# Writing out the order of TensorE and ScalarE ahead of the first pass of a two-layer graph kernel

## The chip, the core and the metric

The kernel runs on one core of one Trainium2 chip. A core has five engines with an instruction queue each: TensorE (PE: matmuls, with weight loads shown apart as PEld), VectorE (DVE), ScalarE (ACT), GpSimd (POOL) and SyncE (SP, which here only issues DMA transfers). Each engine takes its instructions strictly in the order in which they stand in its queue, and waits on semaphores for the others. The metric is the device time of one execution in microseconds (us). The kernel before takes 966.26 us, the median of three runs (964.35 to 967.14).

## The reference

Nodes carry 128 features, there are 6250 of them and 206,250 edges, sorted by destination. Each edge also has a type from 0 to 8. Two layers are computed:

```python
deg  = segment_sum(ones, src);  norm = clip(deg, 1)**-0.5
h    = relu(layernorm(x))
x    = x + relu(segment_sum((h*norm)[src], dst)) @ W0.T + b0          # layer 0
h    = relu(layernorm(x))
msg  = h[src] @ Wmsg.T + bmsg + edge_embed[type]
x    = x + gru(segment_sum(msg, dst), h)                              # layer 1
```

## The kernel before, in words

The edges become a dense matrix of small whole numbers, 6272 by 6272 in blocks of 128 (49 blocks, `NB`). A neighbour sum is then a plain matrix product. Windows of two destination nodes each are handled side by side: an edge list is turned into two one-hot matrices (low seven bits of the source, block number of the source), and TensorE multiplies these to make columns of the dense matrix.

The program has three parts.

**The preparation** (lines 365 to 755) is what the change edits. It goes in stages.

- *Turning the edge lists.* `dst`, `src` and `etype` arrive as 128 x 1616 words (lines 374 to 377). They are cast (`dst_f`, `low_b`, `code_b`, `typ_b`, lines 425 to 435), transposed by matmuls with an identity (line 496) into six PSUM buffers, written to `turned` by ScalarE and VectorE (lines 506, 508), and stored to the DRAM table `flat` (lines 516, 521).
- *Finding the rows.* For each node pair, the place in the edge list where its edges begin is found in two steps: `less` (line 399) and the matmuls into `base_ps` (line 407) find a coarse place by counting the heads of the list, two indirect transfers fetch a `span` of 32 values around it (line 416), and `search`, `search_sums`, `last_of_search` compare and count these (lines 445 to 484). The answer is `row_i`. Between these, `stats(n)` takes the layernorm statistics of n blocks of `x` on VectorE (line 464).
- *The group loop* (lines 734 to 753). There are 25 windows, in groups of `GB` = 4. `fetch` (line 608) lets GpSimd gather the rows of a group (`got`, two buffers, line 612), VectorE compares them with the node numbers (`inside`, line 626) and masks three fields (`fields`, line 633), TensorE transposes these (line 642: 36 matmuls for a group of four windows), ScalarE writes `typ`, `code_t` and `lo_t` (lines 652, 655). `count` (line 659) then counts edge types: nine masks from `typ` (five by VectorE, line 667, four by ScalarE, line 670), ten matmuls into `sums` (lines 671, 672), two copies to `counts` by ScalarE (line 674). A *chunk* is seven blocks of nodes, which are 448 node pairs. `degrees(c)` (line 676) sums the counts of chunk c by seven matmuls (line 681), VectorE reads them (`scale`, `reach`, lines 689, 692) and ScalarE takes a root (line 693). `rows_of(c)` (line 700) makes seven normalised rows, `terms_of(c)` (line 722) rounds them into `tab1[c]`, the table of layer 0.
- *The tail.* `early_hots` (lines 747, 750) makes the first two pairs of one-hot matrices, among the last rows and terms.

**The first pass** (lines 782 to 909) goes over columns of the matrix, 128 in the first step (c = 0) and 256 in each later one. In each round `build` (line 790) makes matrix columns by 32 matmuls (line 801, into three PSUM buffers `ev`), ScalarE copies them to `adj` (line 810), and TensorE multiplies the *previous* step's columns with `tab1` (line 769, 105 matmuls a step, spread evenly over eight rounds of one step).

**The second pass** (lines 915 to 1063) reads the stored matrix again and makes layer 1.

Two things set the order of instructions. A program text in which an engine is named in `tc.manual_schedule` runs on that engine in the order in which it is written. For engines that are not named, a planner chooses the order by its own estimates. In the preparation, only VectorE is named:

```python
with tc.tile_pool(name="pro", bufs=1) as pro, tc.manual_schedule(engines={mybir.EngineType.DVE}):
...
        for i in range(NCH):
            if i >= 3:
                degrees(i - 3)
            fetch(*groups[i])
            if i >= 1:
                count(*groups[i - 1])
            if i >= 3:
                rows_of(i - 3)
                terms_of(i - 3)
```

So VectorE's share of `degrees(c)`, the instructions `scale` and `reach`, stands ahead of `inside` and `fields` of group i = c + 3, while TensorE's and ScalarE's shares stand where the planner puts them. The first pass names TensorE, ScalarE and VectorE all three. GpSimd and SyncE are planned everywhere, before and after.

Of the kernel before, what the change touches and what calls it, by code (L numbers as in the profile page):

```python
# [10 lines left out]
F32 = mybir.dt.float32  # L11
# [247 lines left out]
def by_matrix(  # L259
# [105 lines left out]
    with tc.tile_pool(name="pro", bufs=1) as pro, tc.manual_schedule(engines={mybir.EngineType.DVE}):  # L365
# [40 lines left out]
        for j in range(GT):  # L406
            nc.tensor.matmul(base_ps, less[:, j, :], one_b[:NG, :], start=(j == 0), stop=(j == GT - 1))
        base = pro.tile([P, 1], F32, name="base")
# [14 lines left out]


        dst_f = raw.tile([P, NT], F32, name="dst_f")
        nc.scalar.copy(dst_f, dst_i)
        low_i = raw.tile([P, NT], I32, name="low_i")
        nc.vector.tensor_scalar(low_i, src_i, P - 1, None, op0=ALU.bitwise_and)
# [4 lines left out]
        nc.vector.tensor_copy(code_b, src_i)  # L433
        typ_b = raw.tile([P, NT], BF16, name="typ_b")
        nc.vector.tensor_scalar(typ_b, typ_i, 0.0, float(TYPES - 1), op0=ALU.max, op1=ALU.min)
        row_i = pro.tile([P, WB], I32, name="row_i")
# [51 lines left out]
        for k0 in range(0, NT // P + 1, 4):  # L488
            k1 = min(k0 + 4, NT // P + 1)
            n = min(P, NT - k0 * P)  # L490
            for i, given in enumerate((dst_f, code_b, typ_b, low_b)):
# [17 lines left out]
            if k0 == 0:  # L509
                stats(8)  # L510
            if k0 == 4:
                search()
            if k0 == 8:
                search_sums()
# [90 lines left out]
        groups = [(b, min(GB, WB - b)) for b in range(0, WB, GB)]  # L605
        typ_of = {}

        def fetch(b0_, nb):

            got = wnd.tile([P, GB, ROWS, 4, HALF], I16, name="got")  # L610
            for b in range(nb):
                nc.gpsimd.indirect_dma_start(  # L612
                    out=got[:, b].rearrange("p r f j -> p (r f j)"),
                    out_offset=None,
                    in_=edges_flat,
                    in_offset=bass.IndirectOffsetOnAxis(ap=row_i[:, b0_ + b : b0_ + b + 1], axis=0),
                )
            typ_of[b0_] = wnd.tile([P, GB * WP], BF16, name="typ")
            w0_ = b0_ * WP
            turns_ = {i: pps.tile([P, 4, P], F32, name="turn") for i in (1, 0, 2)}  # L620
            n = nb * ROWS
            g = got[:, :nb].rearrange("p b r f j -> p (b r) f j")
            inside = wnd.tile([P, 2, GB * ROWS, HALF], BF16, name="inside", bufs=1)
            fields = wnd.tile([P, GB * ROWS, 3, 2, HALF], BF16, name="fields")
            for d in range(2):
# [5 lines left out]
                )  # L631
            for d in range(2):
# [5 lines left out]
                )  # L638
            for i in (1, 0, 2):
                for b in range(nb):  # L640
                    for r in range(ROWS):
# [6 lines left out]
                        )  # L648
            for i in (1, 0, 2):
                ws = turns_[i][:, :nb, :WP]  # L650
# [8 lines left out]
        def count(b0_, nb):  # L659
# [4 lines left out]
            for k in range(TYPES):  # L664
                if k < first_level:
                    m = wnd.tile([P, GB * WP], BF16, name="m_dve", bufs=6)
                    nc.vector.tensor_scalar(m[:, :n], typ, float(1 + k), None, op0=ALU.is_equal)  # L667
                else:
                    m = wnd.tile([P, GB * WP], BF16, name="m_act", bufs=4)
                    nc.scalar.activation(m[:, :n], typ, AF.Sign, bias=levels[:, k - first_level : k - first_level + 1])  # L670
                nc.tensor.matmul(sums_t[:both, :n], sel[:, k, :], m[:, :n], start=(k == 0), stop=False)  # L671
            nc.tensor.matmul(sums_t[:both, :n], top, ones_b[:1, :n], start=False, stop=True)
            for d in (0, 1):
                nc.scalar.copy(counts[:, b0_ * WP : b0_ * WP + n, d], sums_t[32 * d : 32 * d + rows3, :n])

        def degrees(c):
            blocks = slice(c * CB, (c + 1) * CB)
            deg = dps.tile([P, CB], F32, name="deg")
            for k in range(CB):
                w = (c * CB + k) * P // 2  # L680
                nc.tensor.matmul(
                    deg[:, k : k + 1],
# [5 lines left out]

            nc.vector.scalar_tensor_tensor(
                scale[:, blocks], deg, 1.0, dev[:, blocks], op0=ALU.max, op1=ALU.mult  # L690
            )
            nc.vector.tensor_copy(reach[:, blocks], deg)
            nc.scalar.activation(scale[:, blocks], scale[:, blocks], AF.Sqrt)

# [5 lines left out]
        def rows_of(c):  # L700

            blocks = slice(c * CB, (c + 1) * CB)
            nc.vector.reciprocal(scale[:, blocks], scale[:, blocks])
            nc.vector.scalar_tensor_tensor(
                shift_[:, blocks], mean[:, blocks], -0.5, scale[:, blocks], op0=ALU.mult, op1=ALU.mult
            )
# [7 lines left out]
            for k in range(CB):  # L714
                b = c * CB + k
                to, of, by, add = f_of[c][:, k, :], xs[:, b, :], scale[:, b : b + 1], shift_[:, b : b + 1]
                if c >= NCH - 3:
                    nc.scalar.activation(to, of, AF.Identity, bias=add, scale=by)
                else:
# [14 lines left out]
        for i in range(NCH):  # L734
            if i >= 3:
                degrees(i - 3)
            fetch(*groups[i])
            if i >= 1:
                count(*groups[i - 1])
            if i >= 3:  # L740
                rows_of(i - 3)
                terms_of(i - 3)
        degrees(NCH - 3)
        count(*groups[NCH - 1])
        rows_of(NCH - 3)
        degrees(NCH - 2)
        early_hots = [hots(0)]
        rows_of(NCH - 2)
        degrees(NCH - 1)
        early_hots.append(hots(TW, first_place[:, NB * P :]))  # L750
        rows_of(NCH - 1)
# [30 lines left out]
    with tc.tile_pool(name="adj_even", bufs=1, reuse_waits="tile") as adj_even, tc.tile_pool(  # L782
# [73 lines left out]
        for c in range(NC + 1):  # L856
# [12 lines left out]
            ends = spread(TOTAL, rounds)  # L869
# [6 lines left out]
            for r in range(rounds):  # L876
                casts = cast_at.get(r, ()) if c > 0 else ()
                for q in casts:
                    if r == 0:
                        cast(q)  # L880
                if c < NC:
# [234 lines left out]
```

## Time and profile before

| what | value |
|---|---|
| median of three runs | 966.26 us |
| the profiled execution, its own time | 970.11 us |
| the profiled execution, span from the first to the last instruction | 968.3 us |
| TensorE, ScalarE, VectorE busy in the span | 886.2, 739.8, 807.8 us |
| mean granted TensorE clock | 0.964 |
| `row_i` written (line 484) | 29.2 us after the start |
| first `inside` (line 626) | 38.2 us |
| first matmul of the first pass' sums (line 769) | 117.08 us |

The page gives busy time by engine, then the span in 40 slices of 24.2 us. In the first five slices TensorE's digits are 4, 3, 5, 6 and 4, and the granted clock's are 9, 6, 7, 7 and 5; from the sixth slice on both are 9 in nearly all slices. The preparation is thus the stretch in which no engine is full all the time. Idle time of an engine that nobody waits for costs nothing, so the busy shares are not enough; the waits and the order of the instructions in time have to be read.

### The profile page before, as it was taken

The page shows a single profiled execution, that of the slowest core. Times are in us where ns is not written, and L with a number is a line of the kernel's source. Part 1 is how long each engine was busy: PE and PEld are TensorE (multiplying, and loading weights), DVE is VectorE, ACT ScalarE, POOL GpSimd, SP SyncE. Part 2 cuts the span into 40 slices and gives each one's busy share as a digit, 9 for nine tenths or more (in the row PEclk, how much of TensorE's full clock was granted, in tenths as well). Part 3 has the DMA queues.
Part 4 walks back from the last instruction along what each step waited for, and adds up shares of the span by engine and source line. Part 5 has one row for each costly group of instructions (what it writes and reads, how often), then busy time and mean ns, then how long its engine had stood idle before and what let it go on. Part 6 is the DMA issues. An engine that isn't in the chain of part 4 may idle for free.

```text
span 968.3 us, 25145 instructions
## 1 busy us (share of the span) xinstructions
PE 886.2 (92%) x11049; PEld 735.5 (76%) x11049; DVE 807.8 (83%) x898; ACT 739.8 (76%) x1407; POOL 35.9 (4%) x73
## 2 busy tenths in 40 slices
PE   4356499999999999999999989999999999999995
PEld 3334399899899999999999878777777777777774
DVE  6969988999999999999999788987887778766753
ACT  3167889999999999999999995767577666667552
POOL 3540000000000000000000000000000000000000
PEclk9677599999999999999999999999999999999998
DMA  9430245575576576576476679877676677565530
GB/s 267 137 96 18 53 130 168 163 207 170 157 206 175 152 206 180 148 206 186 142 206 191 178 260 315 267 250 250 229 256 230 231 260 245 200 227 209 183 88 20
DMA packets 200296, 180.65 MB, mean 187 GB/s; under 512 B 10353, under 2 KB 188583, under 8 KB 200023
## 3 DMA queue, kind: packets, MB, share of 16 engines
q1 hardware_dynamic: 197938, 172.72, 57.5%
q0 software_dynamic: 1664, 4.95, 1.7%
q8 instruction: 88, 1.44, 0.6%
q10 hardware_dynamic: 576, 1.29, 0.4%
q14 instruction: 30, 0.25, 0.1%
HBM read 95.07 MB, written 83.87 MB: 185 GB/s over the span
## 4 chain that ended last, share of the span: by engine, by line
PE 74%; DVE 11%; ACT 7%; DMA 5%; issue 2%; POOL 1%; another core or an unknown queue 0%; SPq 0%; DVEq 0%; ACTq 0%
PE acc L769 52%; PE ev L801 10%; DMA piece<-adj_d 4%; DVE leave L1011 3%; PE turn L642 2%; PE gate L972 2%; PE acc L825 2%; PE gate L973 2%; DVE wide L1038 2%; ACT wide L1031 1%; ACT adj L810 1%; PE sums L671 1%; ACT f L935 1%; PE msg_ps L964 1%; PE tr L953 1%
## 5 line engine op out<-in xcount | busy, mean ns | idle before, releaser
L769 PE MATMUL acc<-wide,tab 128*128 128x256 f32 (+2 forms) x3374 | 600.1, 329 | 3.5 <-DVE wide L1038 3.4
L769 PEld LDWEIGHTS acc<-wide,tab 128*128 128x128 f32 x3374 | 492.0, 189 | 68.2 <-issue 17.7
L810 ACT CAST adj<-ev 128x784 bf16<-128x784 f32 x392 | 298.9, 820 | 30.6 <-PE ev L801 27.6
L1031 ACT ACTIVATE wide<-piece 128x512 fp32r<-128x512 bf16 (+1 forms) x336 | 201.0, 601 | 70.0 <-PE acc L769 64.0
L334 DVE TENSOR_TENSOR hot_l<-lo_t,iota 128x4096 bf16<-128x4096 bf16 x97 | 221.6, 2285 | 0.6 <-PE ev L801 0.5
L1011 DVE TENSOR_REDUCE leave<-piece 128x7 f32<-128x3584 bf16 (+2 forms) x43 | 154.9, 3602 | 47.2 <-DMA piece<-adj_d 47.2
L874 ACT CAST wide<-adj 128x1792 fp32r<-128x1792 bf16 (+1 forms) x75 | 125.2, 1669 | 0.8
L801 PE MATMUL ev<-hot_c,hot_l 64*128 64x49 bf16 x6208 | 114.2, 182 | 7.4 <-DVE hot_c L334 4.2
L801 PEld LDWEIGHTS <-hot_l 64*128 64x128 bf16 x6208 | 93.0, 93 | 36.0 <-issue 8.9
L334 DVE TENSOR_TENSOR hot_c<-code_t,iota 128x1600 bf16<-128x1600 bf16 x97 | 95.5, 985 | 0.0
L1038 DVE CAST wide<-piece 128x3584 fp32r<-128x3584 bf16 (+2 forms) x43 | 82.3, 1921 | 10.4 <-PE acc L769 10.4
L874 DVE CAST wide<-adj 128x1792 fp32r<-128x1792 bf16 (+1 forms) x75 | 81.0, 1079 | 8.7 <-ACT adj L810 7.9
L769 PE MATMUL acc<-adj,tab 128*128 128x256 bf16 x525 | 67.2, 277 | 0.5 <-ACT adj L810 0.5
L1031 ACT ACTIVATION_READ_ACCUMULATOR wide<-piece 128x1 f32 x336 | 63.2, 188 | 0.0
L769 PEld LDWEIGHTS <-tab 128*128 128x128 bf16 x525 | 48.1, 99 | 8.1 <-issue 0.6
L949 ACT COPY sum_sb<-acc 128x512 f32<-128x512 f32 (+2 forms) x13 | 7.3, 562 | 37.4 <-PE acc L769 37.4
L642 PE MATMUL turn<-ident_b,fields 128*128 128x128 bf16 x225 | 20.9, 280 | 15.4 <-DVE fields L633 15.4
L642 PEld LDWEIGHTS <-fields 128*128 128x128 bf16 x225 | 19.9, 131 | 16.1 <-issue 14.0
L612 POOL DMA_INDIRECT got<-flat,row_i x25 | 26.4, 1058 | 23.5 <-DVE m_dve L667 13.6
L972 PE MATMUL gate<-hT,whh_sb 128*128 128x512 f32 (+2 forms) x52 | 25.4, 570 | 1.2 <-DVE hT L961 1.2
L973 PE MATMUL gate<-msg,wih_sb 128*128 128x512 f32 (+2 forms) x52 | 25.3, 567 | 0.0
L980 ACT ACTIVATE rg<-gate,brz 128x512 f32<-128x512 f32 (+2 forms) x13 | 8.6, 664 | 20.0 <-PE gate L973 20.0
(160 smaller groups left out, 558.2 us busy)
## 6 DMA issues: line engine op xcount, KB each, us to landing
adj_d<-adj SPq DMA_DIRECT2D x24, 3136.0 KB
piece<-adj_d SPq DMA_DIRECT2D x77, 896.0 KB
piece<-adj_d SPq DMA_DIRECT2D x14, 672.0 KB
piece<-adj_d SPq DMA_DIRECT2D x7, 448.0 KB
out_dram<-res SPq DMA_DIRECT2D x11, 256.0 KB
xs<-in_x_dram SPq DMA_DIRECT2D x6, 448.0 KB
adj_d<-adj SPq DMA_DIRECT2D x1, 1568.0 KB
flat<-turned SPq DMA_DIRECT2D x3, 512.0 KB
```

The costliest lines, as they stand in the source:

```text
L334: nc.vector.tensor_tensor(to.rearrange("p j (k t) -> p j k t", t=2), twice.unsqueeze(2).to_broadcast([P, n, m // 2, 2]), of[:, :m].rearran ...
L612: nc.gpsimd.indirect_dma_start(out=got[:, b].rearrange("p r f j -> p (r f j)"), out_offset=None, in_=edges_flat, in_offset=bass.IndirectOf ...
L642: nc.tensor.matmul(turns_[i][:, b, :], fields[:, b * ROWS + r, i].rearrange("p d j -> p (d j)"), ident_b, start=(r == 0), stop=(r == ROWS ...
L769: nc.tensor.matmul(acc[:, : 2 * P].rearrange("f (t n) -> f t n", t=2) if twice else acc[:, :nd], tab[:, s, i, :], a[:, i, :P].unsqueeze(1) ...
L801: nc.tensor.matmul(ps[:, d, j * NB : (j + 1) * NB], hot_l[half, t, :], hot_c[half, t, :NB], start=True, stop=True,)
L810: nc.scalar.copy(adj[:, :, part * 16 : (part + 1) * 16].rearrange("p n (j d) -> p n j d", d=2), ps[:, :, : 8 * NB].rearrange("p d (j n) -> ...
L874: make(wide[q][:, :, :n], done[:, q * HP : (q + 1) * HP, :n])
L972: nc.tensor.matmul(ps[:, :nd], whh_sb[:, cols], hT[:, :nd], start=True, stop=False)
L973: nc.tensor.matmul(ps[:, :nd], wih_sb[:, cols], msg[:, :nd], start=False, stop=True)
L1011: nc.vector.tensor_reduce(leave[:, q * HP : (q + 1) * HP, c], piece, AX.X, ALU.add)
L1031: nc.scalar.activation(pieces[q][:, i, :nd], piece[:, i, :nd], AF.Copy, accum_out=leave[:, q * HP + i, c : c + 1],)
L1038: nc.vector.tensor_copy(pieces[q][:, :, :nd], piece[:, :, :nd])
```

## The change

Four edits, all ahead of the first pass but the last.

1. `tc.manual_schedule` of the preparation names TensorE and ScalarE too, so the text has to give them a good order. For this, `fetch` is split into `fetch` (GpSimd alone) and a generator `inside_of`; `count` becomes a generator; `degrees` is split into `degrees`, `scales` and `root`, and `rows_of` loses its first two instructions to `shifts`. A loop calls the pieces in turn.
2. The matmuls that count the heads (`base_ps`, line 407) stand ahead of all transposes. The casts of `dst` and the masking of `low_i` move ahead of `base`, `code_b` is cast by ScalarE in place of VectorE, the four fields are turned in the order `dst_f`, `low_b`, `typ_b`, `code_b`. `search` and `search_sums` come one quarter of the list earlier, with 4 rows of statistics in place of 8.
3. The groups have 2, 4, 4, 4, 4, 4 and 3 windows; they had 4, 4, 4, 4, 4, 4 and 1. In chunks 0 to 3 ScalarE makes 3 of the 7 rows, which VectorE made alone; in chunks 4 to 6 ScalarE makes all seven, as before.
4. In step c = 1 of the first pass, the first 35 of the 105 matmuls (line 769) stand ahead of the first `build`, and none in round 0 after it; the other 70 are spread over the seven rounds left.

```diff
-    with tc.tile_pool(name="pro", bufs=1) as pro, tc.manual_schedule(engines={mybir.EngineType.DVE}):
+    with tc.tile_pool(name="pro", bufs=1) as pro, tc.manual_schedule(
+        engines={mybir.EngineType.PE, mybir.EngineType.Activation, mybir.EngineType.DVE}
+    ):
...
         for j in range(GT):
             nc.tensor.matmul(base_ps, less[:, j, :], one_b[:NG, :], start=(j == 0), stop=(j == GT - 1))
+
+        dst_f = raw.tile([P, NT], F32, name="dst_f")
+        nc.scalar.copy(dst_f, dst_i)
+        low_i = raw.tile([P, NT], I32, name="low_i")
+        nc.vector.tensor_scalar(low_i, src_i, P - 1, None, op0=ALU.bitwise_and)
         base = pro.tile([P, 1], F32, name="base")
...
-        nc.vector.tensor_copy(code_b, src_i)
+        nc.scalar.copy(code_b, src_i)
...
-            for i, given in enumerate((dst_f, code_b, typ_b, low_b)):
+            for i, given in ((0, dst_f), (3, low_b), (2, typ_b), (1, code_b)):
...
             if k0 == 0:
-                stats(8)
+                search()
+                stats(4)
             if k0 == 4:
-                search()
-            if k0 == 8:
                 search_sums()
...
-        groups = [(b, min(GB, WB - b)) for b in range(0, WB, GB)]
+        at = [0, *range(2, WB, GB), WB]
+        groups = [(b, to - b) for b, to in zip(at, at[1:])]
...
-                if c >= NCH - 3:
+                if k in others:
                     nc.scalar.activation(to, of, AF.Identity, bias=add, scale=by)
-                else:
+                elif k in mine_:
                     nc.vector.tensor_scalar(to, of, by, add, op0=ALU.mult, op1=ALU.add)
...
+        ACT_ROWS = 3
+        fetch(*groups[0])
+        for i in range(len(groups)):
+            if i + 1 < len(groups):
+                fetch(*groups[i + 1])
+            new = inside_of(*groups[i])
+            old = count(*groups[i - 1]) if i >= 1 else iter(())
+            c = i - 3
+            run(old, 1)
+            run(new, 1)
+            if c >= 0:
+                degrees(c)
+                scales(c)
+                root(c)
+            run(new, 1)
+            run(old, 1)
+            run(new, 1)
+            if c >= 0:
+                shifts(c)
+                rows_of(c, range(ACT_ROWS, CB), range(ACT_ROWS))
+            run(new, 1)
+            run(old, 2)
+            if c >= 0:
+                terms_of(c)
...
+        old = count(*groups[NCH - 1])
+        run(old, 1)
         degrees(NCH - 3)
-        count(*groups[NCH - 1])
-        rows_of(NCH - 3)
+        scales(NCH - 3)
+        root(NCH - 3)
         degrees(NCH - 2)
+        run(old, 1)
+        shifts(NCH - 3)
+        scales(NCH - 2)
+        root(NCH - 2)
+        rows_of(NCH - 3, (), range(CB))
+        run(old, 2)
         early_hots = [hots(0)]
-        rows_of(NCH - 2)
+        shifts(NCH - 2)
+        rows_of(NCH - 2, (), range(CB))
         degrees(NCH - 1)
+        scales(NCH - 1)
+        root(NCH - 1)
         early_hots.append(hots(TW, first_place[:, NB * P :]))
-        rows_of(NCH - 1)
+        shifts(NCH - 1)
+        rows_of(NCH - 1, (), range(CB))
...
+            lead = (NARROW * SPL + 2) * HP if c == 1 else 0
+            ends = spread(TOTAL - lead, rounds) if c != 1 else [0, *spread(TOTAL - lead, rounds - 1)]
...
+                if r == 0:
+                    run(steps, lead)
                 if c < NC:
```

In the new loop the pieces of `new` (group i) are, in turn: VectorE's `inside`; then VectorE's `fields` and TensorE's transposes; then ScalarE's `typ`; then ScalarE's `code_t` and `lo_t`. The pieces of `old` (counting group i - 1) are ScalarE's four masks; VectorE's five masks; TensorE's ten matmuls; ScalarE's two copies to `counts`. Read engine by engine, an iteration with a chunk is therefore this: VectorE has `inside`, `scale`, `reach`, `fields`, five masks, the two of `shifts`, four rows, the terms. TensorE has the seven matmuls of `degrees`, the transposes, the ten matmuls of `sums`. ScalarE has four masks, the root, `typ`, three rows, `code_t`, `lo_t`, the two copies to `counts`.

## The prediction, made before the result was known

> **What bounds the kernel now.** I read the slices first, then the stage's waits, then the instructions of one iteration in time. Slices (TensorE, ScalarE, granted clock; 24.2 us each):
>
> ```profile
> PE   4356499999999999999999989999999999999995
> ...
> ACT  3167889999999999999999995767577666667552
> ...
> PEclk9677599999999999999999999999999999999998
> ```
>
> From the sixth slice on TensorE is full at the full clock, so the rest of the kernel starts when the preparation lets it and moves with it one to one. Everything below asks when TensorE's unbroken run begins (now 116.31 us, the first `ev` of c = 1). Who waits between 30 and 120 us (total, times, longest):
>
> ```profile
> PE turn L642 <- DVE fields L633: 15.4, 3, 13.5
> ...
> PE deg L681 <- ACT counts L674: 7.1, 5, 2.8
> DVE scale L689 <- PE deg L681: 7.0, 1, 7.0
> ...
> ACT lo_t L655 <- remote: 3.3, 1, 3.3
> ```
>
> VectorE loses 7.0 us once, up to 62.97, waiting for the first degrees. After that it hardly waits: the timeline has `inside` of three groups starting at 73.61, 82.24 and 90.88, that is every 8.6 us, with VectorE busy without a gap. One such iteration, in order of time (start, length):
>
> ```profile
> 82.10 0.16 DVE L689 SCALAR_TENSOR_TENSOR scale<-deg,dev 128x7 f32<-128x7 f32 x1
> ...
> 83.18 2.62 DVE L633 TENSOR_TENSOR fields<-got,inside 128x2304 bf16<-128x2304 int16 x2
> ...
> 84.89 1.42 ACT L674 CAST counts<-sums 27x500 bf16<-27x500 f32 x2
> ...
> 86.36 0.27 PE L681 MATMUL deg<-ones_b,counts 9*128 9x1 bf16 x5 [1.70 <-ACT scale L693]
> ...
> 86.57 3.78 PE L642 MATMUL turn<-ident_b,fields 128*128 128x128 bf16 x36
> ...
> 90.28 1.24 PE L671 MATMUL sums<-m_dve,sel 128*59 128x500 bf16 x5
> ...
> 90.73 0.16 DVE L689 SCALAR_TENSOR_TENSOR scale<-deg,dev 128x7 f32<-128x7 f32 x1
> ```
>
> The point to see: the degrees that VectorE reads at 90.73 were ready at 86.6, some 4 us early. The planner had let TensorE run `degrees` ahead.
>
> **Part by part: the lookup (to 29 us).** `less` ends at 8.26. `base_ps` (0.61) then follows at once and not at 11.34 behind the transposes; `base` and the two places take 0.8, so the two span transfers are issued at 10.2 and 12.5 instead of these:
>
> ```profile
> 12.82 2.03 POOL L416 DMA_INDIRECT span<-in_dst_dram,base_i  x1 [6.42 <-DVE base L422]
> ...
> 15.15 1.64 POOL L416 DMA_INDIRECT span<-in_dst_dram,base_i  x1 [0.30 <-issue]
> ...
> 21.24 1.82 DVE L446 TENSOR_TENSOR is_less<-span,nodes 128x1600 bf16<-128x1600 int32 x1
> ```
>
> By the trace's landing records they completed at 19.58 and 20.98, 6.8 and 5.8 us after issue, while the loads of `x` keep the DMA engines full; with the same delay the second lands at 18.3. `low_i` ahead of `base` costs nothing: `src_i` landed at 5.47, and its 1.0 us hides the matmuls. VectorE gives up `code_b` (1.0) to ScalarE and is through the first quarter at 14.2, so it now waits 4.1 us in `search` for the span. Behind that stand what used to be done meanwhile: 1.8 `is_less`, 0.8 for four rows of statistics, 1.3 second quarter, 2.3 `search_sums`, 1.3 and 0.5 last quarters, 0.3 `row_t`, 2.2 eleven rows, 0.15. `row_i` comes at 18.3 + 10.65 = 28.95, against 29.34: a gain of 0.4. Were the span to land with the `got` delay of 3.3 us (the chain of waits, 38.39), it would be 2.5 more; as late as now, a loss of 2.3. I keep the row of the span itself. The stores of `flat` are not ahead of their old times: SP is issuing loads of `x` up to 16.9. 34 rows of statistics instead of 30 follow (34 x 0.196 = 6.7), then eleven small instructions (2.95): `inside` of group 0 starts at 38.6, was 38.20. The small first group, landed by about 34, is not waited for at all.
>
> **The first groups.** Two windows cost about 0.62 + 1.42 on VectorE (between the rows of one window, 0.42 + 0.82, and of four, 1.03 + 2.62). `fields` of group 0 ends at 40.6 (was 41.76), and frees the buffer for group 2, which takes 7.6 us from there (now 42.03 to the `inside` at 49.68): 48.4. `inside` and `fields` of group 2 end at 52.1. TensorE's stretch on a full group, 36 transposes and ten `sums` matmuls, is the deciding size; I call it x. Four are on the timeline: 57.20 to 62.67, 66.80 to 72.58, 77.22 to 84.53, 86.57 to 92.69, so 5.5, 5.8, 7.3 and 6.1, mean 6.2. It ends at 58.3; two copies to `counts` (1.4), the last `deg` (0.3) and `scale` with `reach` (0.25) bring `fields` of group 3 to 60.2. It is 64.12 now: a gain of 3.9, from the 7.0 us wait.
>
> **The loop.** Here the gain goes. With a first group of two, groups end at 250, 750, 1250, 1750 pairs; chunks end at 448, 896, 1344, 1792. Each of chunks 0 to 3 now reaches into group c + 1 (before, group c sufficed), which is counted at the very end of the previous iteration. And VectorE meets `scale` ahead of `fields`. So the order closes a ring: `fields` 2.6, x 6.2, `counts` 1.4, `deg` 0.3, `scale` 0.25, next `fields`: 10.75 us, with TensorE idle for 4.5 of it. VectorE alone would need 7.8 (8.6 less 3 x 0.27 for the rows given away), ScalarE 8.0 (6.8 + 3 x 0.4): the rows moved to ScalarE lie in waits and are worth nothing. Three turns: `fields` of group 6 starts at 60.2 + 32.2 = 92.4, now 91.21.
>
> [...] The row: transposes follow each other every 0.107 us up to 69.5 and every 0.056 after it, as the granted clock goes from 0.5 to 1.0. [...]
>
> **The tail.** Group 6 has three windows instead of one: `fields` 2.0 and 27 transposes with `sums` of group 5 5.3 (99.7), `counts` 1.4 (101.1). ScalarE then stands with the four masks of group 6 ahead of the root of chunk 4: about 2.15 (between 1.27 for one window and 2.6 for four), 103.3. Root, shifts, `scale`, root: 1.0 (104.3). Seven rows 2.8, `counts` of three windows 1.1, seven rows 2.8, root 0.2: 111.2. VectorE is in the second pair of one-hots until 112.0 and `shifts` until 112.4; the last rows end at 115.2, and only then come all eight `adj` copies (8 x 0.725 = 5.8, from 4.35 for six): 121.0. Now:
>
> ```profile
> 111.08 4.35 ACT L810 CAST adj<-ev 128x784 bf16<-128x784 f32 x6
> ...
> 116.31 0.84 PE L801 MATMUL ev<-hot_c,hot_l 64*128 64x49 bf16 x32 [2.45 <-DVE hot_c L334]
> ```
>
> The copies end at 115.43, two of eight having been done earlier, between rows.
>
> **The 35 matmuls ahead.** They need the copies, not the one-hots, so TensorE starts at 121.05 and not 2.45 us of `hot_c` later: the run begins 4.75 us later than now, this gain counted. In the rounds left TensorE needs 0.58 + 10 x 0.13 = 1.9, ScalarE 1.53 and a cast in some: about 0.4 lost at the end. If one-hots bound, it would be up to 2.
>
> **Sum.** -0.4 (lookup) is inside the chain above, which ends 4.75 + 0.4 = 5.1 later. The profiled span of 968.3 becomes 973.4 (its own time 970.11 becomes 975.2). That execution lies 3.9 above the median 966.26, so the median becomes 971.4.
>
> **Rivals.** *Late completions too.* ScalarE's `lo_t` waited until 53.90 for transposes that by the records ended at 47.86, and once more at 72.11 for some ended at 70.2. I can't say why. Off the ring this cost little; on it, 3.3 and 1.9 us come on top: 976.6. For it: both are in the trace. Against: the two iterations after show none.
> [...]
> [...]
> The edits not being what they say is not a rival I can price: where GpSimd's planned order differs, the lookup's ends above hold it.
>
> **Numbers.** What this kernel's measurement tells from no change is about 0.3%, 2.9 us. The ring as worked out: 0.50, with its own range 968.5 to 975; late completions or the rule's 7.0: 0.18; cancelled 0.15; clock holds 0.17. A little of the first falls within 0.3%: slower 0.64, same 0.19, faster 0.17. Range 962 to 979: it holds the cancelled case, most of the slow ones, and the edge of the fast one.
>
> **What would show it.** Right: between 60 and 95 us VectorE waits on `deg` in `scale` some 2 us in every iteration, `inside` starts 10 to 11 us apart, the `deg` matmuls wait for `counts`, `search` waits 4 us for its transfer, the eight `adj` copies stand in one row. Wrong: `inside` 8.6 us apart or less, or a clock of 1.0 from 45 to 95 us.

## The result, and the profile after

The changed kernel takes 976.43 us (median of four runs, 974.70 to 979.16); the kernel before took 966.21 us in the same series (964.35 to 967.14). The ratio is 1.0111, with a 95% interval of 1.0083 to 1.0139: 10.2 us slower. The prediction was 971.4 us with a range of 962 to 979. The direction was right and the time lies in the range, but only half of the loss was foreseen (5.1 us).

The profiled execution of the changed kernel took 976.74 us by its own time, with a span of 974.7 us. Its page, in slices of 24.4 us (TensorE, ScalarE and the granted clock):

```profile
PE   3356599999999999999999979999999999999995
...
ACT  3277879999999999999999994866667657667562
...
PEclk9587699999999999999999999999999999999998
```

TensorE's fifth digit is a 5 where it was a 4, and from the sixth slice on it is full, as before; slices of 24 us are too coarse to show when the unbroken run begins. The timeline has it: it begins at 119.11 us, with the first of the 35 matmuls, and began at 116.31 before. By the stages below, all but 0.6 us of the difference lies ahead of some 142 us. The waits between 30 and 120 us (total, times, longest):

```profile
PE turn L649 <- DVE fields L639: 25.8, 7, 12.1
...
DVE scale L712 <- PE deg L700: 11.9, 5, 3.7
...
PE deg L700 <- ACT counts L692: 9.0, 6, 2.5
ACT counts L692 <- PE sums L689: 8.0, 6, 2.3
```

VectorE had waited once for degrees, for 7.0 us. Now it waits five times, 11.9 us in all, and the three other rows are the rest of the same circle: `turn` waits for `fields` (12.1 of the 25.8 us are the wait for the very first `fields`), `counts` for `sums`, `deg` for `counts`, and `scale` for `deg`. One turn of it, in order of time (start, length, in brackets the wait just before):

```profile
79.03 1.42 ACT L692 CAST counts<-sums 27x500 bf16<-27x500 f32 x2 [2.34 <-PE sums L689]
80.50 0.20 PE L700 MATMUL deg<-ones_b,counts 9*128 9x1 bf16 x2 [1.31 <-ACT counts L692]
80.74 0.17 DVE L712 SCALAR_TENSOR_TENSOR scale<-deg,dev 128x7 f32<-128x7 f32 x1 [3.15 <-PE deg L700]
80.89 2.62 DVE L639 TENSOR_TENSOR fields<-got,inside 128x2304 bf16<-128x2304 int16 x2
...
83.57 4.02 PE L649 MATMUL turn<-ident_b,fields 128*128 128x128 bf16 x36 [2.87 <-DVE fields L639]
...
88.55 1.22 PE L688 MATMUL sums<-m_dve,sel 128*59 128x500 bf16 x5
...
90.12 1.42 ACT L692 CAST counts<-sums 27x500 bf16<-27x500 f32 x2 [1.51 <-PE sums L689]
91.60 0.17 PE L700 MATMUL deg<-ones_b,counts 9*128 9x1 bf16 x1 [1.29 <-ACT counts L692]
91.81 0.17 DVE L712 SCALAR_TENSOR_TENSOR scale<-deg,dev 128x7 f32<-128x7 f32 x1 [2.49 <-PE deg L700]
```

From `scale` to `scale` it is 11.07 us (91.81 - 80.74). In the kernel before the degrees had been ready 4 us ahead; here each link waits for the one before it.

For the comparison by stage I use a second profiled execution of the kernel before, which the first experiment brought; why, it will show. The predicted column is put together from the prediction's own times.

| stage, us | before, profile shown | before, taken again | predicted | after |
|---|---|---|---|---|
| start to `fields` of group 3 | 64.1 | 61.2 | 60.2 | 58.5 |
| `fields` of group 3 to that of group 6 | 27.1 | 27.1 | 32.2 | 33.5 |
| from there to the end of the eighth `adj` copy | 24.2 | 22.5 | 28.6 | 27.1 |
| from there to the end of the last (105th) matmul of c = 1 | 20.7 | 20.3 | 20.2 | 23.2 |
| the rest of the span | 832.2 | 831.8 | 832.2 | 832.4 |
| span | 968.3 | 962.9 | 973.4 | 974.7 |

Against the undisturbed execution the change gains 2.7 us ahead of the loop, then loses 6.4 in the loop, 4.6 in the tail and 2.9 in c = 1; with 0.6 in the rest this is 11.8 us of span, near the 10.2 us by which the medians differ.

### The profile page after: what moved, and what is told of

It is laid out like the page before. It is cut to its first block, busy times and chain, and to the rows that moved or that the text cites. A ratio compares the mean times of both kernels' runs of the same rounds, so it can differ in the third digit from the quotient of the medians.

```text
span 974.7 us, 25146 instructions
## 1 busy us (share of the span) xinstructions
PE 892.2 (92%) x11049; PEld 738.9 (76%) x11049; DVE 803.3 (82%) x885; ACT 745.4 (76%) x1420; POOL 35.2 (4%) x73
## 4 chain that ended last, share of the span: by engine, by line
PE 73%; DVE 12%; ACT 7%; DMA 4%; issue 2%; POOL 1%; SPq 0%; DVEq 0%; POOLq 0%; ACTq 0%
PE acc L826 51%; PE ev L858 10%; DMA piece<-adj_d 4%; DVE leave L1072 3%; PE turn L649 2%; ACT adj L867 2%; PE gate L1033 2%; PE gate L1034 2%; DVE fields L639 2%; PE acc L882 2%; DVE wide L1099 2%; PE sums L688 1%; ACT f L996 1%; ACT wide L1092 1%; PE msg_ps L1025 1%
## 5 line engine op out<-in xcount | busy, mean ns | idle before, releaser
L858 PEld LDWEIGHTS <-hot_l 64*128 64x128 bf16 x6208 | 92.6, 93 | 31.1 <-issue 8.0
L649 PE MATMUL turn<-ident_b,fields 128*128 128x128 bf16 x225 | 22.3, 289 | 25.8 <-DVE fields L639 25.8
L649 PEld LDWEIGHTS <-fields 128*128 128x128 bf16 x225 | 20.7, 135 | 26.7 <-DVE fields L639 14.5
L664 ACT CAST typ<-turn 128x500 bf16<-128x500 f32 (+2 forms) x7 | 3.7, 532 | 31.0 <-DVE inside L630 24.5
L617 POOL DMA_INDIRECT got<-flat,row_i x25 | 26.5, 1060 | 20.2 <-DVE m_dve L684 10.0
```

Of the source, the lines that this page charges most:

```text
L617: nc.gpsimd.indirect_dma_start(out=got_of[b0_][:, b].rearrange("p r f j -> p (r f j)"), out_offset=None, in_=edges_flat, in_offset=bass.In ...
L649: nc.tensor.matmul(turns_[i][:, b, :], fields[:, b * ROWS + r, i].rearrange("p d j -> p (d j)"), ident_b, start=(r == 0), stop=(r == ROWS ...
L858: nc.tensor.matmul(ps[:, d, j * NB : (j + 1) * NB], hot_l[half, t, :], hot_c[half, t, :NB], start=True, stop=True,)
```

## The experiments

The theory to test (A in the expectations): a ring of dependences, closed by the first group of two, costs the loop and the tail their time; the 35 matmuls ahead of c = 1 cost some 3 us more; and the profile shown of before contained a stall of some 5 us that ordinary executions do not have. They ran in three series, each on a chip of its own and with its own runs of the kernel before; a ratio is always to those. The first has the second profile of before, "without the lead", "groups of four" and "degrees behind"; the second has "only VectorE's part", "the lead alone", "equal groups, no lead" and the first try with added matmuls; the third has the other four. The changed kernel itself was timed only in the measurement above, so every distance to it in time goes across series. Every profile of the second and third series holds such a stall too, so there the stages say more than the times.

**The kernel before, profiled again.** No edit.

> The kernel before, unchanged, for a second profile. The medians differ by 10.2 us (976.4 against 966.2) but the two profiled spans by only 6.4 (974.7 against 968.3). Theory A: the first profiled execution of the kernel before carried a stall of its own (ScalarE's lo_t released at 53.9 us, 6 us after its transposes), which ordinary executions lack. Then in this profile the wait of VectorE for the first degrees is 2 to 4 us instead of 7.0, fields of group 3 starts near 60 instead of 64.1, and the span is near 965. Theory B: the stall belongs to the kernel; it is there again, fields of group 3 starts near 64 and the span is near 968.

It took 964.72 us with a span of 962.9. ScalarE in the timeline of the profile shown of before ("remote" is a release that the trace puts down to no engine of this core):

```profile
53.90 0.99 ACT L655 CAST lo_t<-turn 128x1000 bf16<-128x1000 f32 x1 [3.32 <-remote]
...
60.24 0.58 ACT L652 CAST typ<-turn 128x500 bf16<-128x500 f32 x1
```

The same `typ` of group 2 in the new execution, and then VectorE's `scale` and `fields`:

```profile
55.08 0.57 ACT L652 CAST typ<-turn 128x500 bf16<-128x500 f32 x1 [0.90 <-ACT m_act L670]
...
60.04 0.17 DVE L689 SCALAR_TENSOR_TENSOR scale<-deg,dev 128x7 f32<-128x7 f32 x1 [5.50 <-PE deg L681]
...
61.19 2.62 DVE L633 TENSOR_TENSOR fields<-got,inside 128x2304 bf16<-128x2304 int16 x2
```

The wait put down to "remote" is gone, `typ` of group 2 starts 5.2 us earlier, `fields` of group 3 2.9 and the eighth `adj` copy ends 4.7 us earlier. So one program has executions with and without a stall around 50 to 60 us. The profile shown of before had it; the profile of after has no such wait. Which of the two is the ordinary execution, two profiles can't prove: the 23 runs of before in this series lie between 963.10 and 970.39 us, with the median at 966.95, and this execution lies 2.2 us below that.

**Without the lead.** The 35 matmuls ahead of c = 1 are not set in front; all else is the change.

```diff
-lead = (NARROW * SPL + 2) * HP if c == 1 else 0
-ends = spread(TOTAL - lead, rounds) if c != 1 else [0, *spread(TOTAL - lead, rounds - 1)]
+lead = 0
+ends = spread(TOTAL, rounds)
```

> The changed kernel without its fourth part: in step c = 1 the 105 matmuls are spread over the eight rounds again. Theory A (the 35 matmuls ahead cost time: ScalarE and VectorE stand idle while they run, later the matmuls run into casts that are placed for the old spread, and the clock falls): step c = 1, 23.1 us long in the changed kernel, takes 19.7 as in the kernel before, the run begins 1 us later, so 2 to 2.5 us less than the changed kernel, about 974. Theory B, the prediction's step (they fill the wait for the one-hots and cost 0.4): 0.6 to 1 us more than the changed kernel, about 977.

975.10 us, ratio 1.0079 (1.0052 to 1.0106): 2 to 3 us less than the change (8.2 us above its own median of before, not 10.2; by the ratios 3.1 us), though the intervals overlap. The stage says it better: c = 1 took 21.1 us from the last copy instead of 23.2. The lead costs time and gains none.

**Groups of four from the start.**

```diff
-at = [0, *range(2, WB, GB), WB]
+at = [*range(0, WB, GB), WB]
```

> The changed kernel with the old groups of 4, 4, 4, 4, 4, 4 and 1 windows and nothing else different. Theory A (the first group of two makes each chunk reach into the group counted last, which closes a ring of fields, transposes, sums, counts, degrees and scale): without it VectorE does not wait for degrees, inside starts about 8.3 us apart in place of 10.5 to 11.9, and the time is 6 to 9 us below the changed kernel, 967 to 970. Theory B (the written order itself is slow, ScalarE's queue being the longest): inside stays 10 us apart or more, and the time is within 2 us of the changed kernel.

970.72 us, ratio 1.0042 (1.0031 to 1.0053), which is 6.7 us better than the change. The last three turns of the loop, VectorE's timeline:

```profile
71.05 0.15 DVE L712 SCALAR_TENSOR_TENSOR scale<-deg,dev 128x7 f32<-128x7 f32 x1
71.20 2.61 DVE L639 TENSOR_TENSOR fields<-got,inside 128x2304 bf16<-128x2304 int16 x2
...
80.73 0.17 DVE L712 SCALAR_TENSOR_TENSOR scale<-deg,dev 128x7 f32<-128x7 f32 x1 [0.92 <-PE deg L700]
80.89 2.62 DVE L639 TENSOR_TENSOR fields<-got,inside 128x2304 bf16<-128x2304 int16 x2
...
88.37 0.17 DVE L712 SCALAR_TENSOR_TENSOR scale<-deg,dev 128x7 f32<-128x7 f32 x1
```

The waits of `scale` are 0, 0.92 and 0 where the change has 0, 3.15 and 2.49, and `fields` of group 3 to that of group 6 takes 28.6 us, not 33.5. With equal groups a chunk never reaches into the group that is counted last, and the ring is open. This edit alone brings back 4.9 of the 6.4 us lost in the loop. It brings back part of the tail too, 24.8 us where the change has 27.1 and the undisturbed kernel before 22.5: the last group has one window again and not three. The lead is still in this kernel: c = 1 took 24.8 us.

**Degrees behind the transposes.** In each iteration `degrees`, `scales` and `root` stand behind `fields` and its transposes, not ahead of them.

```diff
+run(new, 1)
 if c >= 0:
     degrees(c)
     scales(c)
     root(c)
-run(new, 1)
 run(old, 1)
```

> The changed kernel, but the degrees, scale and root of a chunk stand behind fields and the transposes of the iteration, not ahead of them; groups of 2, 4, ..., 3 kept. Theory A (the ring through scale sets the iteration): VectorE no longer waits 2.5 to 3.7 us in scale ahead of fields; the iteration is then set by ScalarE's own 8.0 us, so inside starts 8 to 8.5 us apart, and the end comes 8 to 10 us earlier, 966 to 968. Theory B (ScalarE's or TensorE's queue sets it whatever stands where): the wait only moves to another instruction, and the time is within 2 us of the changed kernel.

979.36 us, ratio 1.0120 (1.0095 to 1.0145). The expectation of a gain was missed. The edit made another ring: VectorE's `scale` now waits for `deg` matmuls that stand behind TensorE's 36 transposes, 15.4 us in all, and `inside` starts at 66.90, 79.06 and 91.60, some 12.3 us apart. It was a badly made test, and says only what it cost here that VectorE waits for TensorE directly after giving it 36 transposes.

**Only VectorE's part behind.** `degrees` stays ahead of the transposes, `scales` and `root` go behind `fields`.

```diff
 if c >= 0:
     degrees(c)
-    scales(c)
-    root(c)
 run(new, 1)
+if c >= 0:
+    scales(c)
+    root(c)
```

> The changed kernel, but VectorE's scale and reach, and the root, stand behind fields, while TensorE's degrees stay ahead of the transposes. The run with everything behind the transposes only made another ring: VectorE waited in scale for transposes of its own fields, inside 12.2 us apart. Here neither holds. Theory A (the ring through scale and fields sets the iteration): what is left of it on TensorE and ScalarE is counts 1.4, deg 0.3, transposes and sums 6 to 6.6, so inside starts 8 to 8.6 us apart, fields of group 6 starts 5 to 7 us earlier than 91.97, time 969 to 971. Theory B (in a written order each engine waits for another somewhere, whatever is moved): inside 10 us or more apart, time 975 to 979.

977.58 us, ratio 1.0096 (1.0072 to 1.0121), 1.4 us better than the change's ratio, within the intervals, and not the 969 to 971 expected. The ring is open all the same: the later `inside` are 8.55 and 9.31 us apart, and from `fields` of group 4 to that of group 6 it takes 17.65 us, where the change takes 23.01. But this profile has the stall again (TensorE and ScalarE, in order of time):

```profile
54.99 0.27 PE L649 MATMUL turn<-ident_b,fields 128*128 128x128 bf16 x2 [1.08 <-issue]
56.41 0.37 PE L649 MATMUL turn<-ident_b,fields 128*128 128x128 bf16 x2 [1.15 <-issue]
...
58.57 0.58 ACT L664 CAST typ<-turn 128x500 bf16<-128x500 f32 x1 [1.72 <-remote]
...
63.68 0.99 ACT L667 CAST lo_t<-turn 128x1000 bf16<-128x1000 f32 x1 [1.90 <-remote]
```

`typ` of group 2 comes at 58.57 and not at 53.88, and `fields` of group 4 at 76.07 and not at 68.96. The 5.4 us won in two turns, and more, are lost ahead of them. A kernel further below that has the stall and still the ring ("the lead with the casts moved too") takes 21.6 us for these two turns, so the stall is not what shortened them. Two edits at different links of the ring, this and the equal groups, each shorten the loop: on the path the ring is thus the cause. In the total its price can't be read from this run.

**The lead alone.** The kernel before, with the 35 matmuls put ahead of c = 1 as the change does.

```diff
-ends = spread(TOTAL, rounds)
+lead = (NARROW * SPL + 2) * HP if c == 1 else 0
+ends = spread(TOTAL - lead, rounds) if c != 1 else [0, *spread(TOTAL - lead, rounds - 1)]
...
+if r == 0:
+    run(steps, lead)
```

> The kernel before with the fourth part of the change alone: 35 of the 105 matmuls of step c = 1 ahead of the first build. Theory A (they cost): step c = 1, 20.3 us from the last adj copy to its 105th matmul in the second profile of the kernel before, takes 23 to 25; TensorE waits for a cast in the third round and the clock falls once; 969.5 to 971. Theory B, the prediction's (they fill the 2.45 us wait for the one-hots): 964 to 966.

972.33 us, ratio 1.0030 (1.0015 to 1.0045), that is about 3 us slower; c = 1 took 23.1 us. Its timeline (TensorE, then the three engines behind it):

```profile
114.81 4.64 PE L769 MATMUL acc<-adj,tab 128*128 128x256 bf16 x21 [1.62 <-ACT adj L810]
...
121.78 4.50 ACT L810 CAST adj<-ev 128x784 bf16<-128x784 f32 x6 [6.05 <-PE ev L801]
...
123.06 2.29 DVE L334 TENSOR_TENSOR hot_l<-lo_t,iota 128x4096 bf16<-128x4096 bf16 x1 [3.38 <-PE ev L801]
...
127.17 0.97 PE L769 MATMUL acc<-wide,tab 128*128 128x256 f32 x6 [1.58 <-ACT wide L875]
```

While TensorE works off the lead it makes no `ev`, so ScalarE stands 6.05 us and VectorE 3.38; what they would have done is missing later, and at 127.17 TensorE waits for a cast. The stretch starts earlier and ends later. The fall of the clock that was expected did not come: from 122.95 us on ten `acc<-wide` matmuls take 1.45 to 1.64 us each time, where ten of the changed kernel take 2.14 as its clock falls to 0.50. The lead moves TensorE's matmuls ahead and leaves the casts that feed the others in their old rounds.

**The lead with the casts moved too.** The change, with c = 1's casts one round earlier.

```diff
 cast_at = {0: (1, 2), 2: (3,), 3: (4,), 4: (5,), 5: (6,)}
+CAST_1 = {0: (1, 2, 3), 2: (4,), 3: (5,), 5: (6,)}
...
-casts = cast_at.get(r, ()) if c > 0 else ()
+casts = (CAST_1 if c == 1 else cast_at).get(r, ()) if c > 0 else ()
```

> The changed kernel with the 35 matmuls ahead kept, but the casts of step c = 1 issued sooner: blocks 1, 2 and 3 ahead of the first round, 4 and 5 in the third and fourth. Theory A (the loss of the lead is the wait for casts placed for the old spread, and the clock falling behind it): no wait for a cast in step c = 1, no fall of the clock at 132, the step 23.2 us long becomes 20.5 to 21.5, 974 to 975. Theory B (the loss is that ScalarE and VectorE idle for the 5 us of the lead and have to make it up): the step stays at 22.5 to 23.5 and the time at 976.

979.52 us, ratio 1.0096 (1.0075 to 1.0117), not the 974 to 975 expected. c = 1 took 21.3 us and no longer 23.2; TensorE no longer waits for `wide` in it. The granted clock, which in the change fell to 0.50 from 132.3 to 135.7, shows no such fall: from 132.61 on ten `acc<-wide` matmuls take 1.45 or 1.46 us each time, where in that fall they took 2.14 and 1.90. So 1.9 of the lead's 2.9 us were the casts' place and the clock that fell in the gap. This run alone does not part the two, but the one above speaks for the casts: the lead alone took 23.1 us without any such fall. The time with half clock within c = 1, its beginning included, also differs little: 6.4 us in the change, 3.0 of them at the beginning, and here some 5.7, an estimate from the first 35 matmuls: the 3.0 and twice the 1.34 us by which these take longer here (6.80) than in the change (5.46). Of the 1.9, only 1.4 is in the ratio, well within the intervals, and this profile too had the stall (`fields` of group 3 at 63.90).

**Equal groups, no lead.** Both edits of above together.

> The changed kernel with the old groups and without the 35 matmuls ahead; what is left of the change is the written order, the earlier lookup and ScalarE's three rows. Theory A (the two parts taken away carry the whole loss and add up: 5.7 us by the even groups, and 3 to 4 us by the 24.8 us that step c = 1 took there against 20.3 in the kernel before): 966 to 968, the same as the kernel before. Theory B (the written order loses in the tail on its own): 970 or more.

971.92 us, ratio 1.0046 (1.0029 to 1.0063), where 966 to 968 had been expected. c = 1 took 20.5 us, as in the kernel before, but the total is no better than with equal groups alone. Its profile has the stall: `typ` of group 2 comes at 59.60, `fields` of group 3 at 63.42. The parts don't add up across the two series, and I have no run that says why.

**Equal groups, no lead, `scale` behind `fields`.** The edits of three experiments above together.

> The written order with the old groups, scale behind fields and no matmuls ahead. With even groups only the first chunks waited for degrees (4.9 us in three waits). Theory A (that wait is what is left of the loss of the written order): 1.5 to 3 us below the run with even groups and no lead, the same as the kernel before. Theory B (the rest is in the tail, after the last fields): within 1 us of that run.

972.56 us, ratio 1.0018 (1.0006 to 1.0030). This is the best ratio of the versions with the written order; it is still not faster than the kernel before. Against the one above the step is not clear: by the ratios 2.7 us better, by the distance to its own median of before 1.0 us, from another chip, and its profile ends the eighth `adj` copy at 118.02 where that of the one above has 116.88. So theory A's 1.5 to 3 us are not shown by it. It has the stall (first `scale` at 65.60), and its later `inside` are then some 8.5 us apart, as in the kernel before (8.6).

**TensorE kept busy, first try.** In chunks 0 to 3, 12 matmuls that nobody reads are put ahead of the degrees and 28 behind them, into unused columns of the degrees' own tile.

```diff
-deg_of[c] = dps.tile([P, CB], F32, name="deg")
+deg_of[c] = dps.tile([P, 512], F32, name="deg")
+warm(c, 12)
...
 degrees(c)
+warm(c, 28)
 scales(c)
```

> The changed kernel with matmuls added that nobody reads: in each of chunks 0 to 3, 12 ahead of degrees and 28 behind them, 128 columns each, into unused columns of the bank of deg. They fill TensorE's waits in the ring. Theory A (the fallen clock is what makes the stretch of transposes and sums 5.9 to 7.4 us long instead of 4.5): the granted clock stays at 1.0 from 58 to 92 us, the stretch is 4.5 to 5.0, each iteration 1.5 to 2 us shorter, time 4 to 7 us below the changed kernel, 970 to 972. Theory B (the clock isn't it): the stretch stays above 5.5 and the time is 976 or more, as the added matmuls only cost.

981.79 us, ratio 1.0163 (1.0121 to 1.0206). The time, far from the 970 to 972 of theory A, says nothing about the clock: `scale` reads that tile and waits for the 28 added matmuls as well, and these take 1.74 us in each turn. Its trace says something: the clock is 0.90 from 81 to 92 us and 1.00 from 92 to 107, and the turn in it (`fields` at 88.43 and 99.19) takes 10.8 us; without those 1.7 it would be 9.1.

**TensorE kept busy, second try.** The same matmuls, into the buffer of `sums`, which `scale` doesn't read.

```diff
+warm(c, 12)
 degrees(c)
+warm(c, 28)
 scales(c)
```

> As the run with added matmuls, but these go to the sums buffer of the iteration, which the true matmuls then overwrite. In the earlier run they shared a tile with deg, and VectorE's scale waited for the 28 of them (1.7 us in the ring), so it said nothing on the clock. Theory A (the fallen clock lengthens the stretch): clock at 0.9 to 1.0 from 58 to 92 us, transposes and sums together 4.5 to 5.2 us instead of 5.9 to 7.4, inside 9 to 10 us apart, 971 to 974. Theory B (the stretch has another cause): it stays above 5.5, and the time is 976 or more.

976.24 us, ratio 1.0071 (1.0045 to 1.0097), where 971 to 974 had been expected. By ratio it is 3.9 us better than the change, although it does more (the intervals overlap, and the chips differ). The last two windows of the loop, with busy time of TensorE, its weight loads, VectorE, ScalarE and GpSimd (instructions in parentheses), the granted clock, and DMA share and rate; first of the change:

```profile
60.00:81.00 21.00, 14.01 (x106) 9.98 (x106) 15.94 (x40) 14.77 (x26) 8.59 (x7) 0.76 0.22 67
81.00:105.00 24.00, 16.39 (x113) 10.35 (x113) 16.45 (x46) 17.19 (x35) 0.00 (x0) 0.72 0.00 1
```

and of this experiment:

```profile
60.00:81.00 21.00, 18.43 (x172) 14.98 (x171) 14.89 (x36) 14.50 (x26) 6.46 (x7) 0.66 0.15 48
81.00:105.00 24.00, 19.19 (x219) 13.26 (x217) 18.01 (x49) 20.16 (x37) 0.85 (x1) 1.00 0.06 17
```

With the stall in this profile the first window is worse, then the clock is 1.00 from 81 to 105 us. The transposes of the last turn there:

```profile
88.64 2.18 PE L649 MATMUL turn<-ident_b,fields 128*128 128x128 bf16 x36 [1.20 <-DVE fields L639]
...
92.77 0.39 PE L692 MATMUL sums<-ones_b,top 1*59 1x500 bf16 x1
```

The 36 transposes take 2.18 us, in the turn shown of the change 4.02, and TensorE's whole stretch 4.5 us (88.64 to 93.16) instead of 6.5 (83.57 to 90.08). The turn, from `fields` to `fields`, takes 9.1 us instead of 11.1, as the first try had it. So 2 of this turn's 11 us are the clock, 0.72 in this stretch with the ring's own pauses and 1.00 with them filled. The two turns before it, with a clock of 0.66 from 60 to 81 us, took 11.5 and 10.5 us. All three together are 31.1 us; the kernel with the casts moved, of the same series and with the stall too, takes 33.2. The rest of the ring stays.

**ScalarE's rows under the planner's order.** The kernel before, with ScalarE making three of seven rows in chunks 0 to 3.

```diff
-if c >= NCH - 3:
+if c >= NCH - 3 or k < 3:
```

> The kernel before with one thing of the change alone: ScalarE makes 3 of the 7 rows in chunks 0 to 3 too. Theory A (the loop of the kernel before is VectorE's, 8.6 us a turn without a gap, and ScalarE has room): VectorE's turn shrinks by 3 x 0.27 = 0.8 in four chunks, 2 to 3 us below the kernel before. Theory B (ScalarE's 1.2 us more come into its own queue, and delay counts and degrees): same or up to 2 us slower.

978.56 us, ratio 1.0094 (1.0071 to 1.0118): 8 to 9 us slower, where a gain of 2 to 3 was expected. The timeline of one iteration, ScalarE's rows (`f`) and VectorE's next step:

```profile
69.40 0.50 ACT L718 ACTIVATE f<-xs,shift__464,scale 128x128 f32<-128x128 f32 x1
70.50 0.99 ACT L655 CAST code_t<-turn 128x1000 bf16<-128x1000 f32 x1 [0.61 <-PE turn L642]
73.42 0.99 ACT L655 CAST lo_t<-turn 128x1000 bf16<-128x1000 f32 x1 [1.93 <-PE sums L672]
74.31 0.88 ACT L718 ACTIVATE f<-xs,shift__464,scale 128x128 f32<-128x128 f32 x2
75.22 0.63 DVE L724 TENSOR_SCALAR tab<-f 128x896 bf16<-128x896 f32 x1 [5.29 <-ACT f L718]
```

The planner put one row ahead of `code_t` and `lo_t` and two behind them, and VectorE, which needs all seven, waited 5.29 us here and 3.45 and 2.78 in the next two. `inside` came 11.3 and 10.6 us apart, as in the change but by another wait. The 1.3 us of `f` is not the price; where it stands in ScalarE's queue is.

## Why the prediction was right, and where it was not

**The lookup** was right to 0.1 us: `row_i` done at 28.97 (predicted 28.95), `inside` of group 0 at 38.69 (38.6), `fields` of group 0 done at 40.65 (40.6). `search` (its first instruction is `is_less`) waited 4.63 us for its span where 4.1 was foreseen:

```profile
18.55 1.82 DVE L448 TENSOR_TENSOR is_less<-span,nodes 128x1600 bf16<-128x1600 int32 x1 [4.63 <-DMA span<-in_dst_dram,base_i]
```

The landing time of the old row, 5.8 us from issue, was nearer than the 3.3 us of `got`: in the change the two spans landed 6.1 and 6.6 us after issue.

**The ring** was right in its place, its links and nearly its size: turns of 10.5, 11.9 and 11.1 us, predicted 10.75. The kernel with equal groups shows that the first group of two closes it, and the one with `scale` behind `fields` that VectorE's order is the other half. The stretch x on TensorE (36 transposes and ten matmuls into `sums`) was 4.5 ahead of the loop, with a granted clock of 1.00 from 50.3 to 60.6, where the prediction had 6.2: that is the 1.7 us by which the loop began earlier than foreseen. Then it was 5.9, 7.4 and 6.5: mean 6.6 in the loop, against the 6.2 that the prediction took from four stretches of before, and 0.4 more in each of three turns is nearly the 1.3 us by which the loop was mis-sized. With the pauses filled x was 4.5, at a clock of 1.00 from 81 to 105 us where the change had 0.72; so the rest of x goes with the clock. What sets the moment at which the clock falls no run shows: at 132.3 us in the change it fell from 1.00 to 0.50 while TensorE was working, 1.92 us after the end of a pause of 1.58.

**The rows on ScalarE** were costed at nothing, because they lie in VectorE's waits. In the changed kernel no run took this part away, so that is not shown by itself. Under the planner's order the same rows cost 8 to 9 us: the price of such a move is not its duration.

**The tail** took 27.1 us; 28.6 was predicted. I had all eight `adj` copies behind the last rows. ScalarE did two of them ahead (first copies at 110.58, then six at 114.70), as it had in the kernel before:

```profile
110.58 1.53 ACT L867 CAST adj<-ev 128x784 bf16<-128x784 f32 x2
...
114.70 4.35 ACT L867 CAST adj<-ev 128x784 bf16<-128x784 f32 x6
...
119.11 3.86 PE L826 MATMUL acc<-adj,tab 128*128 128x256 bf16 x21 [1.63 <-ACT adj L867]
```

**The matmuls ahead** failed: "about 0.4 lost at the end" was 2.9. I counted TensorE's work in the rounds left and ScalarE's casts, and not what is no longer done while the lead runs. The kernel before with the lead alone shows about 3 us (ratio 1.0030; c = 1 takes 23.1 us), and taking the lead out of the change brings back 2.1 of the 2.9 in the stage. c = 1 in the change has the same three waits as there:

```profile
124.99 4.50 ACT L867 CAST adj<-ev 128x784 bf16<-128x784 f32 x6 [4.96 <-PE ev L858]
...
126.27 2.29 DVE L334 TENSOR_TENSOR hot_l<-lo_t,iota 128x4096 bf16<-128x4096 bf16 x1 [2.04 <-PE ev L858]
...
130.38 0.97 PE L826 MATMUL acc<-wide,tab 128*128 128x256 f32 x6 [1.58 <-ACT wide L933]
```

**The step from the profile to the median** failed, and cost most. The forecast for the profiled execution was 975.2 us; it took 976.74, 1.5 more. That this is so near is luck in part: the lead was 3.0 and the loop 1.3 us too small, what stands ahead of the loop 1.7 and the tail 1.5 too large, with 0.2 in the rest and 0.2 outside the span. To come to the median I took off 3.9 us, since the profiled execution of before lay that far above its median. The execution of after lay only 0.3 above its own: 3.5 of the missing 5.0 us are this step. The second profile of before shows why: the first held a stall, in the stretch where I replaced the old wait of 7.0 us by a path of my own, worked out from ordinary durations. My path had no stall in it, so the stall was taken off twice: once within the "gain of 3.9, from the 7.0 us wait", of which it was 2.9 (`fields` of group 3 at 64.1 and 61.2), once in the step to the median. Against the undisturbed execution of before, which has 5.5 us in that wait, the path gave a gain of 1.0; measured were 2.7, by the shorter x. That the stall is the whole excess of 3.9 is not shown: no execution of before at its median has a profile.

**The rivals.** "Cancelled" and "clock holds" did not come: the change is 10.2 us slower, and the clock was 0.76 from 60 to 81 us and 0.72 from 81 to 105. No run shows the 7.0 us for x, or a rule behind it, that the chances name; in the loop x was 5.9, 7.4 and 6.5. "Late completions" gave 976.6, next to the measured time, but by a mechanism that was not there: the profile of after has no such wait. That its number is near is no support for it.

**What stays open** is the stall itself. In the profiles it is absent in the second execution of before, in the change and in the other three kernels of the first series; it is there in the profile shown of before and in all eight kernels of the second and third series, which ran on other chips. The kernel before had medians of 966.95, 968.98 and 970.63 us in the three series, which goes with it but does not show that the chip decides. How much it costs each kernel is not known, so ratios of different series may be compared only roughly, and several of the gains above (`scale` behind `fields`, the early casts) are seen in their stage and not clearly in the time. Open too is the rest of the tail: in the three profiles with equal groups it is still 1.3 to 2.3 us longer than in the undisturbed execution of before, and no run parts that.

## What to carry to other kernels

Where the profiled execution lies above the median by more than the runs scatter, find the stretch in which it is long before a wait there is booked as something to gain; the excess is otherwise counted twice. When an order is written out by hand, ask of each consumer into which batch it reaches, and whether that batch is what the loop makes last: a batch boundary moved by half was enough to turn a spare 4 us into a ring. And when work is moved ahead on one engine, what feeds the rest of it has to move too, and the engines that live from what it used to make in that time stand idle (ScalarE 6.05 us and VectorE 3.38 with the lead alone).

## What the runs showed of the hardware that was not expected

In two cases ScalarE, waiting for TensorE's transposes, started 6.0 and 1.8 us after these had ended by the records: in the first profile of before `lo_t` started at 53.90 us, its transposes had ended at 47.86; with `scale` behind `fields`, `typ` started at 58.57, its transposes had ended by 56.78 at the latest. In the latter profile the matmuls themselves also come two or three at a time, 1.4 us apart (54.99 and 56.41 us). The same program has executions with and without this stall (964.72 and 970.11 us). And adding 40 matmuls a turn that are never read made a turn at the full clock shorter, not longer, once they were out of the way of `scale`: 9.1 us, against 11.1 with pauses. The kernel's time did not get worse by it (ratio 1.0071, the change 1.0111, from different series).
